# Reordering small steps of a pre-norm attention and mixture-of-experts kernel: clears on another queue, an exponential behind a copy, scatters moved and tied

## The chip, the cores and the metric

The kernel runs on one core of a Trainium2 chip. A core has a matrix engine (PE), a vector engine (DVE), a scalar engine (ACT), GpSimd (POOL) and a sync engine (SP) that only issues transfers; 16 DMA engines carry all transfers. The engines run side by side and wait for each other through semaphores. The metric is the time of one execution on the device in microseconds (us); the lower, the better. "Row" is one of the 8 sequences of the batch, numbered 0 to 7, and "tile (b, j)" is the j-th of the eight blocks of 128 tokens of row b, numbered 0 to 63 in all.

## What is computed

The input x has 8 rows of 1024 tokens with 128 features. The reference, cut to what matters:

```python
x = x + attn(layernorm(x), Wq, Wk, Wv, Wo)      # 16 heads of 8, window of 64 tokens
x = x + ffn(layernorm(x), w_router, w1, w2, bias)

# ffn: T = 8192 tokens, E = 8 experts, two experts a token, capacity 2048 an expert
scores = softmax(xf @ w_router)
expert_weights, top_experts = top_k(scores, 2)
order = argsort(flat_e, stable=True)             # a token's slot: its rank in its expert
xb = zeros((E * capacity + 1, hs)).at[slot].set(xf[src])
h = gelu(einsum('ech,ehf->ecf', xb, w1))
y = einsum('ecf,efh->ech', h, w2)
out = zeros((T, hs)).at[src].add(flat_w[order][:, None] * yv) + bias
```

So each token's normalized features are scattered to a slot of each of its two experts, in the order of the tokens, and the experts' results are added back to the tokens.

## The kernel before

The kernel has two stages. In the first, a loop over the 64 tiles does the attention and, a row later, the routing of the finished row; in the second, eight experts run over their 2048 slots each.

The attention of a tile: `scores` (L524) forms products of queries and keys on PE, and DVE takes their maxima (L565). `turn_max` turns the maxima on PE, and ACT copies them (L584). `probs` (L589) forms the products again the other way round, with the maxima subtracted (L602 to L626), and ACT takes two exponentials (L632, 1.0 us each). `attend` (L638) multiplies by the values on PE (L647), and ACT copies the result, the context and its denominators, out of PSUM (L655). In tile i the loop at L1156 issues the scores of tile i + 2, the `attend` of tile i - 1 and the `probs` of tile i. `Context` (L660) sends denominators and context by SP into another layout, where DVE inverts and scales them (L704, L705). Before a row can start, its x is normalized (`first`, L923), turned (`turn`), multiplied into queries, keys and values, and queries and keys are copied apart by SP (`spread`, L492: eight copies for each half of a row).

The order of work on PE, DVE, ACT and POOL is written out by hand: each of these engines runs its instructions in the order of the code. SP isn't in that list (L125): a planner orders its transfers by when it expects them to be ready. Three kinds of loads are held back by an explicit dependency (`after`, L92), and a tile's list `plan[i]` holds the small steps beside the attention. Of each list, what comes before the second step with a PE product runs in tile i behind `probs`; the rest, `behind`, runs in tile i + 1, after its scores and before its `attend`. The list `pairs[i]` runs in tile i + 1 between `attend` and `probs`.

The routing of a row b - 1 (class `Piece`, L750) runs in row b: `out` (the output projection), `stats`, `root` (the inverse square root by three Newton steps), `rooted`, `softmax` (whose exponential on ACT is L821), `choose` twice (the two best experts), `count` (PE counts the tokens of each expert, L857), `place` (slots, starting at L869), `slots` (indices for the scatters). In row b's tile 4, `rooted` and `softmax` are in `plan`, so they run in tile 5 ahead of the copy L655. `keep` (L804) adds the bias to the row on GpSimd and writes it to the output by SP.

GpSimd has three kinds of work. The scatters (`put`, L896, instruction L902) each write 128 tokens to `xb` in HBM; there are 128, taken in order from a queue, up to two a tile in rows 0 to 4 and three from row 5 on, each behind a named PE instruction. The second is the root of the row after next (L391 to L399), which is in `plan` of tile 2 behind the second product and so runs in tile 3, after that tile's first scatter. The third is `keep`. Ahead of all scatters `xb` must be cleared: `clears` (L310) writes zeros in 16 transfers of 528 KB, issued by ACT, one a tile in tiles 1 to 13 and then two a tile. The zeros themselves are made by GpSimd at 17 us.

At the end, row 7 is routed in two pieces of four tiles (`piece`, L1047, stepped by `go`). Behind the last `attend`, all scatters left over are issued, then the first piece's eight, then the second piece's eight; the second stage reads `xb` only when all are in.

Of the kernel before, what the change touches and what calls it, by code (L numbers as in the profile page):

```python
# [48 lines left out]
def kernel(  # L49
# [66 lines left out]
    with ExitStack() as ph:  # L116
# [193 lines left out]
        def clears():  # L310

            half = CAP // 2
            for i in range(2 * E):
                to = xb[i * half : (i + 1) * half, :].rearrange("(p n) d -> p (n d)", p=P)
                nc.scalar.dma_start(
                    out=to.rearrange("p (m k) -> p m k", m=NS // 8),
                    in_=bc_mid(zeros.rearrange("p n d -> p (n d)"), NS // 8),
                )
                yield
# [430 lines left out]
        class Piece:  # L750
# [47 lines left out]
            def rooted(self):  # L798
                self.norm.rooted()
# [4 lines left out]
            def keep(self):  # L804

                for j in range(0, self.n, 2):
                    t0, rows = self.b * L + (self.j0 + j) * P, self.rows[:, j : j + 2]
                    on = nc.vector if self.alone else nc.gpsimd
                    on.tensor_tensor(rows, rows, bc_mid(bias_sb, 2), ALU.add)  # L809
                    nc.sync.dma_start(  # L810
                        out=acc[t0 : t0 + 2 * P, :].rearrange("(j p) d -> p j d", p=P), in_=rows
                    )

            def softmax(self):
# [5 lines left out]
                nc.vector.tensor_tensor(self.pe, self.pe, bc(self.lmx, E), ALU.subtract)  # L820
                nc.scalar.activation(self.pe, self.pe, AF.Exp)  # L821

            def choose(self, k):
# [18 lines left out]
                if k == 0:  # L842
                    nc.vector.scalar_tensor_tensor(
                        pe, oh, -2.0, pe, op0=ALU.mult, op1=ALU.add
                    )
                else:
                    self.both = self.small("both", E)
                    nc.vector.tensor_tensor(
                        self.both, self.hot[:, :, 0], self.hot[:, :, 1], ALU.add
                    )  # L850
# [89 lines left out]
        def of(b, j0, what, *args):  # L940
            getattr(seconds[b, j0], what)(*args)
# [6 lines left out]
        at(0, 0, first, 1, "stats")  # L948
        at(0, 1, first, 1, "root", nc.vector)
        at(0, 1, first, 1, "rooted")  # L950
        at(0, 1, first, 1, "apply", range(NJ))
        at(0, 1, turn, 1, 0)
        at(0, 2, values, 0, 2)
        at(0, 2, queries, 1, 0)
        at(0, 3, keys, 1, 0)
        at(0, 3, spread, 1, 0)
        at(0, 3, first, 2, "stats")
        at(0, 3, turn, 1, 1)
        at(0, 4, queries, 1, 1)
        at(0, 4, first, 2, "root", nc.gpsimd)  # L960
        at(0, 5, keys, 1, 1)
        at(0, 5, values, 1, 0)
        at(0, 6, first, 2, "rooted")
# [6 lines left out]
        for b in range(1, B):  # L970
# [32 lines left out]
            for t, what, *args in (  # L1003
# [3 lines left out]
                (n + 4, "slots"), (n + 4, "keep"),  # L1007
            ):
                plan[t].append((of, (*f, what, *args)))
            for i in range(4):  # L1010
                pairs[n + i].append(partial(of, *f, "apply", range(2 * i, 2 * i + 2)))
            plan[n + 3][:0] = [(of, (*f, "count")), (of, (*f, "place"))]


        def half(b, j0, *steps):
# [8 lines left out]
                (of, *f, "softmax"),  # L1024
                (of, *f, "apply", FOUR[0]),
# [16 lines left out]

        half(6, 0, (53, 2), (54, 2), (55, 1), (56, 4), (57, 2), (58, 3))
        half(6, 4, (57, 2), (58, 2), (59, 1), (60, 4), (61, 2), (62, 3))


        def piece(j0, j1):  # L1047
# [8 lines left out]
                (of, *f, "softmax"),  # L1056
                (of, *f, "choose", 0),
# [5 lines left out]
                (put, 3 if j0 else 8),  # L1063
# [4 lines left out]
        def go(steps, n):  # L1068
            for _, (call, *args) in zip(range(n), steps):
                call(*args)  # L1070
                n -= 1
            return n == 0
# [4 lines left out]
        at(7, 7, go, ends[0], 4)  # L1077
# [78 lines left out]
        for i, (b, j) in enumerate(tiles):  # L1156
# [8 lines left out]
            def scores_ahead():  # L1165
                if i + 2 < len(tiles):
                    put(1, scores(*tiles[i + 2]))
# [42 lines left out]
        for which, n in ((0, 2), (1, 2), (0, 3), (1, 9), (0, 1), (1, 2)):  # L1210
            go(ends[which], n)

# [153 lines left out]
```

## Time and profile before

| | us |
|---|---|
| median of three runs | 763.94 (762.25 to 768.26) |
| the profiled execution | 764.12 |
| its span, first to last instruction | 762.3 |
| PE busy in the span | 637.5 |
| DVE, ACT, POOL busy | 381.9, 363.7, 375.7 |
| first attention exponential (L632) starts | 26.5 |
| last one starts (two, 1.94 together) | 444.5 |
| last scatter into `xb` starts | 493.2 |
| first expert's product on PE | 498.4 |

In the profile, an engine's busy time is the time of its own instructions; idle time is named by what ended it. A line such as "[9.14 <-DMA den<-sums]" behind an instruction says that its engine stood 9.14 us before it and that a transfer from `sums` to `den` ended the wait. PEclk is the share of its full clock that PE was granted.

### The profile page before, as it was taken

To read this page: it belongs to the slowest core of one execution; us is meant where nothing else is said; L and a number is where in the kernel's file an instruction comes from. 1 tells how busy PE (TensorE), PEld (TensorE's weight loads), DVE (VectorE), ACT (ScalarE), POOL (GpSimd) and SP (SyncE) were. 2 spreads that over 40 slices of the span, in tenths; PEclk is the share of its full clock that TensorE was granted. 3 is DMA by queue.
4 is the path that set the end of the run, shared out by engine and by line. 5 is a ranking of instruction groups with operands and counts; after the bars stand their busy time and mean duration, and the time that the engine had idled before them with its cause. 6 is when DMAs were issued, how large, how long until landed. Compare 5 with 4: busy or idle time off the path is not lost.

```text
span 762.3 us, 21779 instructions
## 1 busy us (share of the span) xinstructions
PE 637.5 (84%) x8777; PEld 470.3 (62%) x8777; DVE 381.9 (50%) x1169; ACT 363.7 (48%) x637; POOL 375.7 (49%) x431
## 2 busy tenths in 40 slices
PE   8797897989989888798887651499999999999990
PEld 7454554645545545455554430489999999898990
DVE  6754687766787778587888864221111111111010
ACT  5274556656656665475564530023444444443430
POOL 7010011342534435423424437538778787787876
PEclk9999798998999999999999975699999999999995
DMA  2444545333333434323332111146456465463433
GB/s 75 136 161 140 179 144 194 97 104 106 95 107 112 134 102 129 102 84 118 98 96 88 51 50 53 59 125 108 47 115 106 46 121 89 58 117 34 38 31 30
DMA packets 78308, 74.00 MB, mean 97 GB/s; under 512 B 13907, under 2 KB 63928, under 8 KB 77312
## 3 DMA queue, kind: packets, MB, share of 16 engines
q1 hardware_dynamic: 50944, 46.94, 20.0%
q0 software_dynamic: 22528, 16.74, 15.9%
q10 hardware_dynamic: 4736, 8.93, 3.1%
q8 instruction: 69, 1.13, 0.7%
q14 instruction: 31, 0.25, 0.1%
HBM read 19.14 MB, written 30.28 MB: 65 GB/s over the span
## 4 chain that ended last, share of the span: by engine, by line
PE 48%; DVE 12%; issue 11%; ACT 8%; POOL 6%; DMA 6%; SPq 6%; another core or an unknown queue 1%; POOLq 0%; ACTq 0%; DVEq 0%
PE hp L1274 12%; PE yp L1285 12%; PE av L647 6%; ACT pr L632 5%; PE t L619 5%; POOL out_dram L1295 4%; DVE mx L565 3%; PE s L557 2%; ACT mxt L584 2%; PE po L781 2%; DMA out_dram<-ye,dest 2%; PE t L602 2%; SPq L678 2%; PE xt L1263 2%; PE t L626 1%
## 5 line engine op out<-in xcount | busy, mean ns | idle before, releaser
L1295 POOL DMA_INDIRECT out_dram<-ye,dest x128 | 197.8, 1545 | 66.1 <-issue 27.1
L902 POOL DMA_INDIRECT xb<-xn,si x128 | 126.0, 985 | 169.9 <-PE s L557 58.3
L632 ACT ACTIVATE pr<-t 128x1024 f32<-128x1024 f32 x128 | 123.9, 1020 | 51.6 <-PE t L626 38.0
L565 DVE TENSOR_REDUCE mx<-s 128x8 f32<-128x768 f32 x128 | 116.4, 952 | 52.9 <-PE s L557 52.7
L1285 PEld LDWEIGHTS yp<-w,hT 128*128 128x128 f32 x1024 | 124.1, 192 | 9.2 <-ACT hT L1278 6.1
L1285 PE MATMUL yp<-w,hT 128*128 128x128 f32 x1024 | 125.3, 275 | 4.4 <-DVE ye L1290 3.7
L1274 PE MATMUL hp<-xts,w 128*128 128x256 f32 (+1 forms) x528 | 121.7, 373 | 0.3 <-DVE xts L1265 0.3
L1278 ACT ACTIVATE hT<-hp 128x512 f32<-128x512 f32 x128 | 76.4, 597 | 68.2 <-PE hp L1274 64.2
L1290 DVE TENSOR_TENSOR ye<-yp,gt 128x256 f32<-128x256 f32 (+1 forms) x66 | 27.1, 415 | 160.6 <-PE yp L1285 128.0
L1274 PEld LDWEIGHTS hp<-xts,w 128*128 128x128 f32 x528 | 93.3, 190 | 10.2 <-DVE xts L1265 0.6
L655 ACT COPY sums<-av 128x512 f32<-128x512 f32 x63 | 36.9, 586 | 92.6 <-PE av L647 59.6
L647 PE MATMUL av<-pr,vbd 128*32 128x128 f32 x2016 | 72.9, 287 | 3.7 <-ACT mxt L584 2.1
L619 PE MATMUL t<-qbd,kt 32*128 32x256 f32 x1024 | 73.9, 390 | 0.0
L647 PEld LDWEIGHTS av<-pr,vbd 128*32 128x32 f32 x2016 | 54.5, 114 | 24.7 <-ACT mxt L584 9.6
L557 PE MATMUL s<-kbd,qt 32*32 32x384 f32 x2048 | 62.6, 518 | 1.3 <-DMA kbd<-kt 1.3
L1265 ACT COPY xts<-xt 128x256 f32<-128x256 f32 (+1 forms) x57 | 21.0, 369 | 87.8 <-PE xt L1263 83.2
L619 PEld LDWEIGHTS t<-qbd,kt 32*128 32x128 f32 x1024 | 51.3, 193 | 3.4 <-issue 1.1
L809 POOL TENSOR_TENSOR x<-x,bias_sb 128x256 f32<-128x256 f32 x28 | 20.4, 752 | 49.8 <-ACT xn L415 48.5
L391 POOL TENSOR_SCALAR ln_h_x<-ln_v_x 128x8 f32<-128x8 f32 x6 | 1.5, 246 | 87.3 <-DVE ln_v_x L384 87.3
L541 PE MATMUL s<-ms,i 32*128 32x256 bf16 x256 | 29.8, 282 | 14.6 <-ACT pr L632 10.9
L704 DVE RECIPROCAL den<-den 128x128 f32<-128x128 f32 x39 | 36.8, 944 | 9.8 <-DMA den<-sums 8.3
L541 PEld LDWEIGHTS <-i 32*128 32x128 bf16 x256 | 10.3, 91 | 48.1 <-issue 43.5
(185 smaller groups left out, 785.0 us busy)
## 6 DMA issues: line engine op xcount, KB each, us to landing
xb<-zeros ACTq DMA_DIRECT2D x16, 528.0 KB
xe<-xb SPq DMA_DIRECT2D x7, 1056.0 KB
vbd<-vbd SPq DMA_DIRECT2D x32, 192.0 KB
kbd<-kt SPq DMA_DIRECT2D x62, 72.0 KB
qbd<-qt SPq DMA_DIRECT2D x64, 64.0 KB
out_dram<-x SPq DMA_DIRECT2D x32, 128.0 KB
w<-in_L_ffn_w_dram SPq DMA_DIRECT2D x16, 256.0 KB
x<-in_L_attn_x_dram SPq DMA_DIRECT2D x22, 128.0 KB
```

The lines of the kernel that those rows point to most:

```text
L541: nc.tensor.matmul(ends_of, lhsT=i32[quad(g), 0:4, :].rearrange("p n q -> p (n q)"), rhs=ms[quad(g)], start=True, stop=False, skip_group_c ...
L557: done = nc.tensor.matmul(place(g, slice(32 * blk, 32 * (blk + 1))), lhsT=qt[quad(g), q0 : q0 + 32], rhs=kbd[quad(g), :, c0 + 32 * blk : c ...
L565: nc.vector.tensor_reduce(out=part_of(mx, 0)[:, 2 * u : 2 * u + 2], in_=units[u][:, :, 0 : 4 * KB].rearrange("p g (r k) -> p g r k", r=4), ...
L619: nc.tensor.matmul(units[g // 2][:, g % 2, w], lhsT=kt[quad(g), q0 : q0 + P], rhs=qbd[quad(g), :, c0 : c0 + 64], start=False, stop=False, ...
L632: nc.scalar.activation(pr[:, 2 * u : 2 * u + 2], units[u], AF.Exp)
L647: last = nc.tensor.matmul(av[quad(g), k, :, w], lhsT=pair_values(vbd, 2 * j + w, g, k), rhs=pr[:, g, w, 2 * k : 2 * k + 2, :], start=True, ...
L655: nc.scalar.copy(sums[b, j // 4][:, :, j % 4], av.rearrange("p k s w q -> p (k s) (w q)"))
L902: ins = nc.gpsimd.indirect_dma_start(out=xb[:, :], out_offset=bass.IndirectOffsetOnAxis(ap=slot, axis=0), in_=row, in_offset=None, bounds_ ...
L1274: nc.tensor.matmul(hp[:, c], lhsT=ws[e][0][:, (c0 + c) * P : (c0 + c + 1) * P], rhs=xt, start=True, stop=True,)
L1278: nc.scalar.activation(hT[:, c0 : c0 + per], hp, AF.Gelu_apprx_tanh)
L1285: nc.tensor.matmul(yp[:, k, :], lhsT=hT[:, c, k * P : (k + 1) * P], rhs=ws[e][1][:, c, :], start=c == 0, stop=c == NC - 1,)
L1295: add = nc.gpsimd.indirect_dma_start(out=acc, out_offset=bass.IndirectOffsetOnAxis(ap=dests[e][:, n : n + 1], axis=0), in_=ye[:, k, :], in ...
```

## The change

- The 16 clears are issued by SP instead of ACT.
- `softmax` is cut in two: the exponential L821 becomes a step of its own, `exp`, and stands at the head of `pairs[n]`, behind the next tile's copy L655.
- `count` stays at the head of tile 7's list; `place` moves to its end, and so into the next tile.
- `keep` does two of the eight blocks in each of four tiles instead of all in one.
- In rows 1 to 5, tile 3's scatter behind the scores is left out; in row 5 also tile 3's scatter behind the context. Tile 6 gets one more behind the context in rows before 5.
- In row 0, the steps that prepare row 1 and the root of row 2 are spread over later tiles.
- At the end, `go` returns the last instruction of the steps it ran, and of the first piece's eight scatters two stand as before, two wait for the second piece's `rooted`, two for its `softmax`, two for the first `choose`.

```diff
-                nc.scalar.dma_start(
+                nc.sync.dma_start(
                     out=to.rearrange("p (m k) -> p m k", m=NS // 8),
...
-            def keep(self):
-
-                for j in range(0, self.n, 2):
+            def keep(self, tiles=None):
+
+                for j in tiles or range(0, self.n, 2):
...
-                nc.vector.tensor_tensor(self.pe, self.pe, bc(self.lmx, E), ALU.subtract)
+                return nc.vector.tensor_tensor(self.pe, self.pe, bc(self.lmx, E), ALU.subtract)
+
+            def exp(self):
                 nc.scalar.activation(self.pe, self.pe, AF.Exp)
...
-        at(0, 0, first, 1, "stats")
-        at(0, 1, first, 1, "root", nc.vector)
-        at(0, 1, first, 1, "rooted")
-        at(0, 1, first, 1, "apply", range(NJ))
-        at(0, 1, turn, 1, 0)
+        at(0, 1, first, 1, "stats")
         at(0, 2, values, 0, 2)
-        at(0, 2, queries, 1, 0)
+        at(0, 2, first, 1, "root", nc.vector)
+        at(0, 2, first, 1, "rooted")
+        at(0, 2, first, 1, "apply", FOUR[0])
+        at(0, 2, turn, 1, 0)
+        at(0, 3, queries, 1, 0)
+        at(0, 3, first, 1, "apply", FOUR[1])
         at(0, 3, keys, 1, 0)
         at(0, 3, spread, 1, 0)
-        at(0, 3, first, 2, "stats")
-        at(0, 3, turn, 1, 1)
+        at(0, 4, turn, 1, 1)
+        at(0, 4, first, 2, "stats")
         at(0, 4, queries, 1, 1)
-        at(0, 4, first, 2, "root", nc.gpsimd)
         at(0, 5, keys, 1, 1)
+        at(0, 5, first, 2, "root", nc.gpsimd)
         at(0, 5, values, 1, 0)
-        at(0, 6, first, 2, "rooted")
+        at(0, 7, first, 2, "rooted")
...
-                (n + 4, "slots"), (n + 4, "keep"),
+                (n + 4, "slots"),
+                (n + 4, "keep", (0,)), (n + 5, "keep", (2,)),
+                (n + 6, "keep", (4,)), (n + 7, "keep", (6,)),
             ):
                 plan[t].append((of, (*f, what, *args)))
+            pairs[n].append(partial(of, *f, "exp"))
...
-            plan[n + 3][:0] = [(of, (*f, "count")), (of, (*f, "place"))]
+            plan[n + 3].insert(0, (of, (*f, "count")))
+            plan[n + 3].append((of, (*f, "place")))
...
-                    put(1, scores(*tiles[i + 2]))
+                    put(0 if 1 <= b < 6 and j == 3 else 1, scores(*tiles[i + 2]))
...
-                put(1 if b >= 5 else 0, begun)
+                put(1 if b >= 5 and (b > 5 or j != 3) or j == 6 else 0, begun)
...
-        for which, n in ((0, 2), (1, 2), (0, 3), (1, 9), (0, 1), (1, 2)):
+        for which, n in ((0, 2), (1, 2), (0, 2)):
             go(ends[which], n)
+        put(2)
+        for n in (2, 1, 2):
+            put(2, go(ends[1], n))
+        put(len(puts), go(ends[1], 2))
+        go(ends[1], 3)
+        put(3)
+        go(ends[0], 1)
+        go(ends[1], 1)
```

More of the change, by code (lines that the diff above doesn't have):

```diff
@@ L798, in rooted @@
             def rooted(self):
-                self.norm.rooted()
+                return self.norm.rooted()
             def apply(self, tiles):
                 self.norm.apply(self.rows, self.xe2[:, :, 0:D], tiles)
-            def keep(self):
-                for j in range(0, self.n, 2):
+            def keep(self, tiles=None):
+                for j in tiles or range(0, self.n, 2):
                     t0, rows = self.b * L + (self.j0 + j) * P, self.rows[:, j : j + 2]
@@ L842, in choose @@
                 if k == 0:
-                    nc.vector.scalar_tensor_tensor(
+                    return nc.vector.scalar_tensor_tensor(
                         pe, oh, -2.0, pe, op0=ALU.mult, op1=ALU.add
                     )
[L846 to L850, printed above, removed]
+                self.both = self.small("both", E)
+                return nc.vector.tensor_tensor(
+                    self.both, self.hot[:, :, 0], self.hot[:, :, 1], ALU.add
+                )
             def count(self):
@@ L940, in of @@
         def of(b, j0, what, *args):
-            getattr(seconds[b, j0], what)(*args)
+            return getattr(seconds[b, j0], what)(*args)
         at(0, 0, queries, 0, 1)
@@ L1024, in half @@
                 (of, *f, "softmax"),
+                (of, *f, "exp"),
                 (of, *f, "apply", FOUR[0]),
@@ L1041, in half @@
             assert not calls
-        half(6, 0, (53, 2), (54, 2), (55, 1), (56, 4), (57, 2), (58, 3))
-        half(6, 4, (57, 2), (58, 2), (59, 1), (60, 4), (61, 2), (62, 3))
+        half(6, 0, (53, 2), (54, 2), (55, 1), (56, 5), (57, 2), (58, 3))
+        half(6, 4, (57, 2), (58, 2), (59, 1), (60, 5), (61, 2), (62, 3))
         def piece(j0, j1):
@@ L1056, in piece @@
                 (of, *f, "softmax"),
+                (of, *f, "exp"),
                 (of, *f, "choose", 0),
@@ L1062, in piece @@
                 (of, *f, "slots"),
-                (put, 3 if j0 else 8),
                 (of, *f, "keep"),
@@ L1069, in go @@
             for _, (call, *args) in zip(range(n), steps):
-                call(*args)
-                n -= 1
-            return n == 0
+                done = call(*args)
+            return done
         ends = [piece(0, 4), piece(4, 8)]
@@ L1076 @@
         at(7, 6, go, ends[0], 3)
-        at(7, 7, go, ends[0], 4)
+        at(7, 7, go, ends[0], 5)
         at(7, 7, go, ends[1], 2)
```

## The prediction

> **What bounds the kernel now.** I read the page first (busy rows, chain, groups), then the waits, then the timeline by tile, taking the start of each tile's probability exponential (ACT L632) as its beat.
>
> Page, kernel before:
>
> ```profile
> span 762.3 us, 21779 instructions
> PE 637.5 (84%) x8777; PEld 470.3 (62%) x8777; DVE 381.9 (50%) x1169; ACT 363.7 (48%) x637; POOL 375.7 (49%) x431
> q10 hardware_dynamic: 4736, 8.93, 3.1%
> ```
>
> PE carries the span, but not evenly. From 498 us the expert stage runs (264 us, and the diff doesn't touch it). Calm attention tiles beat at 5.64 to 5.72 us; the 64 tiles from 26.5 to 450 us take about 6.6 each. The excess is waiting, and the waits name it (engine and line, waited for; us in total, times, longest):
>
> ```profile
> ACT sums L655 <- DMA den<-sums: 12.3, 2, 9.1
> ACT lg L821 <- DVE lg L820: 33.9, 8, 13.9
> DVE upto L869 <- PE pc L857: 11.4, 8, 2.8
> ACT pr L632 <- remote: 5.9, 1, 5.9
> ```
>
> Each is a place the change touches. The first, in order of time (start, length, engine, line; idle before and releaser in brackets):
>
> ```profile
> 68.28 0.59 ACT L584 COPY mxt<-pm 128x512 bf16<-128x512 bf16 x1
> ...
> 74.83 2.47 SPq L676 DMA_DIRECT2D den<-sums  x4
> 77.45 0.52 ACTq L315 DMA_DIRECT2D xb<-zeros  x1
> 78.02 0.59 ACT L655 COPY sums<-av 128x512 f32<-128x512 f32 x1 [9.14 <-DMA den<-sums]
> ```
>
> ACT stands 9.14 us in front of one clear, which waits for a completion counter that an SP transfer (74.83) still holds; the context's copy L655 queues behind it. The second, in row 3's tile 5:
>
> ```profile
> 217.10 1.08 PE L647 MATMUL av<-pr,vbd 128*32 128x128 f32 x32
> 220.42 0.23 DVE L820 TENSOR_TENSOR lg<-lg,lmx 128x64 f32<-128x64 f32 x1
> 220.68 0.26 ACT L821 ACTIVATE lg<-lg 128x64 f32<-128x64 f32 x1 [2.88 <-DVE lg L820]
> 220.99 0.59 ACT L655 COPY sums<-av 128x512 f32<-128x512 f32 x1
> ```
>
> The copy could start at 218.2, when PE is done; it stands behind the logits' exponential until 220.99.
>
> **The change, part by part.** Sums are made against the profiled execution: 764.12 us, its span of 762.3 and 1.8 around it; the median of the runs shown is 763.94, so both read alike.
>
> *Clears on SP.* ACT loses 16 issues of 0.52 us and, above all, the waits in front of them. By the beats: tile 6 to 7 takes 12.04 against 5.7 (6.3), 7 to 8 takes 7.50 against 6.6 in the same place of rows 3 and 4 (0.9), 14 to 15 takes 7.38 against 5.6 (1.8), 15 to 16 takes 8.37 against 6.6 (1.8): together 10.8 us. What they cost on SP has no row. SP isn't ordered by hand: the copies of kt for row 2 go out at 129.50, before the values' transfer at 135.67 that stands earlier in the code; and the loads of x and w are held back by an explicit dependency. The clears have none but `zeros` (17.5 us), so I expect them in SP's first gaps (19.4 to 22.3, 23.7 to 28.5, 33.4 to 40.7) instead of one per tile. q10 carried 8.93 MB in 3.1% of 762.3 us, 23.6 us; a clear of 528 KB is 1.43 us of all engines, 16 are 23. Behind some 12 of them (17 us from 19.4; SP's transfers use eight completion counters in turn, so only eight are open at once) the eight copies of `spread(0, 1)`, issued at 28.5 to 33.4, would land near 44 rather than 35; scores of tile 4 read them at 39.0: 5 us. Bounds: 0 (the planner spaces them, or they fit the gaps), and 16 (all 16 ahead of the values' pair of 22.27, which the context at 33.6 reads: 11, and the copies behind it, 5). I take 5.5, by the gaps above. Net -5.3; bounds -10.8 and +5.2.
>
> Here the Trainium skill speaks against the edit. *DMA: Bandwidth & Descriptors* ("Issuing engines are not separate DMA queues") says that another issuing engine saves only the issue time: by it the gain is 16 x 0.52 = 8 us of an engine that is 48% busy, next to nothing. Its section "Queues, rings and completion order" says that engines take turns between queue rows, but keep order within one: by it a copy behind a clear now waits for all of it, where before both advanced. The row says that the saving is not issue time: 9.14 us at one clear. On the second rule the trace has no row for a clear ahead of a copy; my 5.5 is that rule's price.
>
> *The exponential behind the copy.* In each of rows 0 to 5 (their logits come a row later) the copy (0.59, next start 0.48 later) moves out from behind the exponential, but the exponential still stands ahead of the two `apply` and of the next L632: ACT's order becomes copy, wait to 220.68, exponential (0.31 to the next start), applies (0.78), L632 at 221.77 instead of 222.25. So not the 2.3 us of the copy's lateness, but 0.5, six times: -3.0. PE's queries, which wait 1.68 for the copy's buffer, come earlier at no cost. Bounds 0 (PE is late elsewhere) and -5 (row 2's slower beat after it, 7.7 against 5.7, goes too).
>
> *Scatters and GpSimd's root.* In rows 2 to 5 the scatter taken away in tile 3 is issued before the root (203.93; root from 206.48, waiting for DVE), so those behind the root stay two in rows 2 to 4:
>
> ```profile
> 210.89 1.06 POOL L902 DMA_INDIRECT xb<-xn,si  x1 [0.57 <-issue]
> 212.26 0.97 POOL L902 DMA_INDIRECT xb<-xn,si  x1 [0.30 <-issue]
> 213.03 0.59 ACT L655 COPY sums<-av 128x512 f32<-128x512 f32 x1 [3.16 <-PE t L626]
> ```
>
> PE had ended av at 211.18; ACT saw it 1.85 us late. Back-to-back scatters go with late releases, here and in row 5, where four of them (313.2 to 318.1) go with 5.9 us at L632. There the change takes one of the four: I take 1.5, a quarter. Bounds 0 and -6. The scatter given back in tile 6 stands between others 0.7 us apart: 0 taken, +2 at most. In row 5 the counts still end at 16 in tile 6, so 13 scatters are left at the end as before.
>
> *`place` behind the values, `keep` in four.* DVE waits 1.57 us for the counts in tile 7 and then needs 1.4 for `place`, so the maxima (L565, 237.21) come 1.8 after their scores and PE loses 0.66. That goes; but `place`'s 1.4 us then lies ahead of `slots` and the maxima in the next tile, where DVE has no gap. GpSimd's four additions in a row (241.03, 2.88 us) go with a DVE product of 0.91 us that elsewhere takes 0.29; one per tile spares 0.6. I take -1; bounds -5 and +3. Rows are kept up to three tiles later, so loads of x into the same buffers start later; they have a row's time: 0 (or +2 if SP stands before one).
>
> *Row 0's start.* The statistics of row 1 (DVE, 1.41 us at 30.23) leave the tile where PE waits 1.68 for maxima; root and half the normalizing move a tile on; row 1's queries and keys half a tile to a tile, their copies to SP with them, still ahead of tile 6. I take -1; bounds -3 and +2.
>
> *The end.* Thirteen scatters hold GpSimd from 452.2, then eight of the first piece to 478.8, then it idles until the second piece's slots (483.35). DVE's chain steps there at 0.70 or 1.40 us instead of 0.23:
>
> ```profile
> 475.63 0.19 DVE L834 TENSOR_REDUCE xn<-lg 128x4 f32<-128x32 f32 x1 [0.51 <-DVE lg L843]
> 476.34 0.19 DVE L836 TENSOR_TENSOR rk<-lg,xn 128x32 f32<-128x32 f32 x1 [0.52 <-DVE xn L834]
> ...
> 484.10 1.09 POOL L902 DMA_INDIRECT xb<-xn,si  x1 [5.31 <-issue]
> ```
>
> The new ties hold two scatters each for the root's end (466.7), the softmax (467.4) and the first choice (475.1); in the old run those scatters start at 471.4, 473.96 and 476.52. All three are then met, so nothing moves, unless fewer scatters at once let DVE step faster: then GpSimd, back to back, is the bound, 484.1 minus 479.1 = 5 us. Queued behind a tied scatter stand only later scatters. I take -0.8; bounds -5 and +2.
>
> Sum: -5.3 - 3.0 - 1.5 - 1 - 1 - 0.8 = -12.6, 764.1 to 751.5.
>
> **The rivals.** *Nothing gained in sum:* SP gives back what ACT gains (11 us), and only the exponential and half the rest stays: 759. For it: half-clock time follows every early wait (granted clock 0.90 from 34 to 137 us). Against: the wait at 78 us is single and large, and early tiles have idle PE.
>
> *Better:* SP's gaps hold the clears at 2 us, row 5's wait goes by 4, the end by 4: 764.1 - 8.8 - 3 - 4 - 2 - 4 = 742; with row 2 and the start as well, 738.
>
> *Slower:* SP becomes the bound in rows 0 and 1. It issues about 56 transfers a row at 0.6 us, 34 of some 50 us; the clears add 8 us of issue, and each can hold the queue until the transfer eight before it has landed, up to 16 x 1.43 = 23 in all. Copies, values and denominators then come late to PE by up to 31, of which early slack takes 10. That is +21 against -10.8 and -3: 771. It decides once SP costs more than some 18 us.
>
> **How the numbers follow.** Forecast (742 to 757) 0.50; better (738 and below to 742) 0.16; nothing in sum (757 to 765) 0.18; slower 0.16. About 1% (7.6 us) is what a measurement of this kernel can tell from no change. Faster by over 1%: 0.66; within: 0.18; slower: 0.16. The range leaves out the lower half of "better" and most of "slower": 738 to 767.
>
> **What would show it.** No ACT wait on a transfer before L655 in rows 0 and 1; clears on SP before 60 us; the kt copies of row 0 landing near 44; L632 of tile 5 half a microsecond sooner after L820 in each row; row 5's tile 4 still late, by about 4; last slots within 2 us of L632's last beat as before. Wrong if SP spaces the clears, if back-to-back scatters aren't what delays releases, or if DVE's slow steps at the end go.

## The result, and the profile after

The kernel after takes 766.57 us (median of 19 runs, 763.21 to 770.88), the kernel before, beside it, 762.25 (19 runs, 759.01 to 768.26): a ratio of 1.005, 95% interval 1.0031 to 1.0069. It is 3.8 us slower (2.4 to 5.3), where 12.6 us of gain were forecast. The profiled execution took 767.43 us.

The page of after, the lines that answer to those of before:

```profile
span 765.6 us, 21779 instructions
PE 638.2 (83%) x8777; PEld 471.0 (62%) x8777; DVE 382.6 (50%) x1169; ACT 363.6 (47%) x637; POOL 375.8 (49%) x431
q10 hardware_dynamic: 384, 0.28, 0.1%
```

Busy times are the same; the clears have left ACT's queue. The expert stage takes 263.4 us (263.2 before), so the difference lies in the attention. By rows, from the first L632 of a row to the next row's, before and after (one profile each): 59.5 to 62.4, 51.2 to 49.7, 52.5 to 51.2, 50.1 to 50.9, 50.1 to 54.8, 56.2 to 53.0, 51.5 to 51.2, 46.9 to 49.1; then from the last tile to the first expert 54.6 to 53.3.

The waits of after (engine and line, waited for; us in total, times, longest):

```profile
ACT pr L632 <- PE t L626: 49.1, 34, 9.6
ACT sums L655 <- remote: 23.9, 8, 3.8
DVE ctx L705 <- DMA ctx<-sums: 17.4, 13, 2.9
DVE den L704 <- DMA den<-sums: 15.2, 9, 5.0
DVE one L688 <- DMA one<-total: 10.0, 5, 4.7
```

ACT's 12.3 us for "den<-sums" are gone from this list. In their place VectorE waits longer for the same kind of transfer: 15.2 for den (8.3 before), 17.4 for ctx (9.6), 10.0 for one (2.9), and the copies L655 wait 23.9 us for a release that the profile can't name (5.1). (A release is the moment at which an engine learns through a semaphore that the product or transfer it waits for is done; one that comes later than the end of that product is called late here.) In the profile of before, VectorE's wait for den lies under ACT's:

```profile
78.61 0.95 DVE L704 RECIPROCAL den<-den 128x128 f32<-128x128 f32 x1 [4.90 <-DMA den<-sums]
```

The timeline of tiles (0,6) and (0,7) after shows the first exchange:

```profile
78.44 2.47 SPq L676 DMA_DIRECT2D den<-sums  x4
78.70 0.58 ACT L655 COPY sums<-av 128x512 f32<-128x512 f32 x1 [0.69 <-PE av L647]
...
82.22 0.95 DVE L704 RECIPROCAL den<-den 128x128 f32<-128x128 f32 x1 [4.96 <-DMA den<-sums]
84.83 0.29 DVE L705 TENSOR_TENSOR ctx<-ctx,den 128x128 f32<-128x128 f32 x1 [1.66 <-DMA ctx<-sums]
85.04 1.82 DVE L565 TENSOR_REDUCE mx<-s 128x8 f32<-128x768 f32 x2
86.05 0.58 PE L610 MATMUL t<-i,mt 32*128 32x128 bf16 x11 [7.20 <-DVE mx L565]
...
88.92 1.94 ACT L632 ACTIVATE pr<-t 128x1024 f32<-128x1024 f32 x2 [9.64 <-PE t L626]
```

ACT no longer stands in front of a clear; its copy runs at 78.70 after 0.69 us. But SP sends den only at 78.44, VectorE's scaling waits 4.96 us for it, the maxima stand behind the scaling, PE waits 7.20 for the maxima, and ACT waits 9.64 for PE. Tile (0,6) falls from 12.04 to 4.86 us, tile (0,7) rises from 7.50 to 13.84.

And in SP's list of after, with PE's wait behind it (of the 16 clears eight stand ahead of the copies of queries and keys, six behind them):

```profile
24.46 7.55 SPq L315 DMA_DIRECT2D xb<-zeros  x6
...
38.63 0.59 SPq L499 DMA_DIRECT2D kbd<-kt  x1
...
40.68 1.40 PE L557 MATMUL s<-kbd,qt 32*32 32x384 f32 x32 [3.59 <-DMA kbd<-kt]
```

This is the price that the prediction had put on the clears. Tile (0,1) takes 9.98 us instead of 5.64; as row 0's new order shortens tile (0,0) from 11.26 to 9.17, the two together take 2.3 us more (19.15 against 16.90).

Row 3 of after, tiles 3 to 6 (start, length, engine, line), and under it the two lines of before for the maxima of tile 5:

```profile
206.51 1.76 SPq L496 DMA_DIRECT2D qbd<-qt  x3
211.01 1.09 POOL L903 DMA_INDIRECT xb<-xn,si  x1 [0.58 <-PE av L647]
212.11 0.75 POOL L809 TENSOR_TENSOR x<-x,bias_sb 128x256 f32<-128x256 f32 x1
212.51 1.94 ACT L632 ACTIVATE pr<-t 128x1024 f32<-128x1024 f32 x2 [0.93 <-PE t L626]
212.89 0.38 SPq L810 DMA_DIRECT2D out_dram<-x  x1
213.03 0.99 POOL L903 DMA_INDIRECT xb<-xn,si  x1 [0.17 <-issue]
213.80 0.93 PE L557 MATMUL s<-kbd,qt 32*32 32x384 f32 x32
214.32 0.97 POOL L903 DMA_INDIRECT xb<-xn,si  x1 [0.30 <-issue]
216.26 1.82 DVE L565 TENSOR_REDUCE mx<-s 128x8 f32<-128x768 f32 x2 [1.14 <-PE tp_x L436]
217.41 2.17 SPq L673 DMA_DIRECT2D total<-sums  x4
...
221.45 1.91 ACT L632 ACTIVATE pr<-t 128x1024 f32<-128x1024 f32 x2
222.41 0.46 SPq L683 DMA_DIRECT2D one<-total  x1
224.26 0.97 POOL L903 DMA_INDIRECT xb<-xn,si  x1 [4.14 <-PE s L557]
225.54 0.97 POOL L903 DMA_INDIRECT xb<-xn,si  x1 [0.30 <-issue]
227.40 0.59 ACT L655 COPY sums<-av 128x512 f32<-128x512 f32 x1 [2.98 <-remote]
```

```profile
215.34 0.93 PE L557 MATMUL s<-kbd,qt 32*32 32x384 f32 x32
216.42 1.82 DVE L565 TENSOR_REDUCE mx<-s 128x8 f32<-128x768 f32 x2 [1.14 <-PE s L557]
```

Four readings. The release behind the root that was 1.85 us late in before is gone: a bias addition (212.11) now stands between the scatters, and tile 3 takes 5.80 instead of 7.08. The pair of scatters now stands at 213.03 and 214.32, and the scores that end at 214.73 reach VectorE only at 216.26, 1.53 us late (0.15 in the same place of before). SP issued three qbd copies at 206.51 and then stands until 212.89, when GpSimd has added: the write of the row holds back the fourth qbd copy, the keys, total (217.41) and one (222.41). And tile 6's given back scatter makes another pair (224.26, 225.54), with a copy that waits 2.98. Row 3 in sum: 0.8 us longer. The largest loss of a single row is row 4's 4.7 us; no lines of it are shown, but the parts below tell where it comes from: row 4 takes 55.3 us with the additions alone (e4) and 50.5 when their last write is held back (f3), against 50.1 in before.

### The profile page after: what moved, and what is told of

It reads as the page before. It is cut to its first block, busy times and chain, and to the rows that moved or that the text cites. A ratio compares the mean times of both kernels' runs of the same rounds, so it can differ in the third digit from the quotient of the medians.

```text
span 765.6 us, 21779 instructions
## 1 busy us (share of the span) xinstructions
PE 638.2 (83%) x8777; PEld 471.0 (62%) x8777; DVE 382.6 (50%) x1169; ACT 363.6 (47%) x637; POOL 375.8 (49%) x431
## 3 DMA queue, kind: packets, MB, share of 16 engines
q8 instruction: 69, 1.13, 0.7%
## 4 chain that ended last, share of the span: by engine, by line
PE 32%; issue 15%; POOL 12%; DVE 12%; ACT 11%; DMA 9%; SPq 7%; another core or an unknown queue 1%; POOLq 0%; DVEq 0%; ACTq 0%
POOL out_dram L1310 11%; ACT pr L632 7%; PE av L647 5%; PE t L619 5%; DMA out_dram<-ye,dest 5%; PE yp L1300 5%; PE hp L1289 4%; PE awake L169 3%; DVE mx L565 3%; SPq L678 2%; ACT mxt L584 2%; SPq L676 2%; PE po L781 2%; PE t L602 2%; DMA ctx<-sums 2%
## 5 line engine op out<-in xcount | busy, mean ns | idle before, releaser
L903 POOL DMA_INDIRECT xb<-xn,si x128 | 125.9, 984 | 199.7 <-PE t L626 49.3
L632 ACT ACTIVATE pr<-t 128x1024 f32<-128x1024 f32 x128 | 123.8, 1019 | 54.1 <-PE t L626 49.1
L565 DVE TENSOR_REDUCE mx<-s 128x8 f32<-128x768 f32 x128 | 116.3, 951 | 44.4 <-PE s L557 40.4
L1305 DVE TENSOR_TENSOR ye<-yp,gt 128x256 f32<-128x256 f32 (+1 forms) x66 | 27.0, 415 | 160.7 <-PE yp L1300 128.6
L655 ACT COPY sums<-av 128x512 f32<-128x512 f32 x63 | 36.8, 585 | 99.1 <-PE av L647 68.9
L619 PE MATMUL t<-qbd,kt 32*128 32x256 f32 x1024 | 78.0, 398 | 1.1 <-issue 1.0
L619 PEld LDWEIGHTS t<-qbd,kt 32*128 32x128 f32 x1024 | 53.6, 195 | 5.4 <-issue 3.2
L704 DVE RECIPROCAL den<-den 128x128 f32<-128x128 f32 x39 | 36.8, 945 | 15.2 <-DMA den<-sums 15.2
L541 PE MATMUL s<-ms,i 32*128 32x256 bf16 x256 | 28.1, 280 | 16.3 <-ACT pr L632 12.5
L602 PE MATMUL t<-i,mt 32*128 32x256 bf16 x448 | 28.9, 281 | 14.6 <-DVE mx L565 9.3
```

The source lines that it names most:

```text
L541: nc.tensor.matmul(ends_of, lhsT=i32[quad(g), 0:4, :].rearrange("p n q -> p (n q)"), rhs=ms[quad(g)], start=True, stop=False, skip_group_c ...
L565: nc.vector.tensor_reduce(out=part_of(mx, 0)[:, 2 * u : 2 * u + 2], in_=units[u][:, :, 0 : 4 * KB].rearrange("p g (r k) -> p g r k", r=4), ...
L602: nc.tensor.matmul(to, lhsT=mt[quad(g), 0, hq, :], rhs=i32[quad(g)].rearrange("p (w r) q -> p w r q", w=2), start=hq == 0, stop=False, ski ...
L619: nc.tensor.matmul(units[g // 2][:, g % 2, w], lhsT=kt[quad(g), q0 : q0 + P], rhs=qbd[quad(g), :, c0 : c0 + 64], start=False, stop=False, ...
L632: nc.scalar.activation(pr[:, 2 * u : 2 * u + 2], units[u], AF.Exp)
L903: ins = nc.gpsimd.indirect_dma_start(out=xb[:, :], out_offset=bass.IndirectOffsetOnAxis(ap=slot, axis=0), in_=row, in_offset=None, bounds_ ...
```

## The experiments

Each set of runs ran on one chip with the kernel before beside it; all ratios are against that. Before took 763.5 to 765.2 us in four sets and 744.94 on the chip of e9 to e12, called the faster chip below. Ratios are turned to us with the set's own before. "Beat 3 to 4" is from the start of L632 in a row's tile 3 to that in tile 4; a beat comes from one profile.

### One part at a time

The first seven each do one part of the change on the kernel before, or (e7) undo one in after.

**Clears on SP** alone:

```diff
-                nc.scalar.dma_start(
+                nc.sync.dma_start(
```

> Kernel before with one edit: the 16 clears are issued by SP. Prediction's step: 5.3 us faster than before (ACT's waits of 10.8 us gone, some 5 us at the copies of kt). Theory A, after the result: the wait at ACT only lay over a backlog of SP that is there anyway, so it moves: tile (0,6) falls from 12.0 to about 5, tile (0,7) rises by as much (DVE's first scaling of the context waits for the same transfer), tile (0,1) is 4 us longer; in sum +1 to +5 us. Rival B, SP becomes the bound of row 1 too: rows 0 and 1 together longer by more than 6 us.

Measured: 763.94 against 763.47, ratio 1.0008 (0.9976 to 1.0040). Tile (0,6) takes 4.86 us, (0,7) 12.70, (0,1) 9.62: theory A's mechanism. By the profiles, tiles (0,0) and (0,1) are 2.5 us longer together, (0,6) and (0,7) 2.0 shorter. In row 1 tiles 6 and 7, which took 7.38 and 8.37, take 5.06 and 6.64: there the 3.6 us of the prediction come. The row is 1.6 us shorter, as tiles 0 and 5 of it got longer.

**The exponential behind the copy** alone:

```diff
-                nc.vector.tensor_tensor(self.pe, self.pe, bc(self.lmx, E), ALU.subtract)
+                return nc.vector.tensor_tensor(self.pe, self.pe, bc(self.lmx, E), ALU.subtract)
+
+            def exp(self):
                 nc.scalar.activation(self.pe, self.pe, AF.Exp)
...
+            pairs[n].append(partial(of, *f, "exp"))
```

> Kernel before with one edit: the logits' exponential stands behind the context's copy. Prediction's step: 3.0 us faster (0.5 in each of rows 0 to 5). Rival: the copy's earlier end lets PE and GpSimd's scatter go earlier, and what follows waits anyway; no difference (within 1.5 us), with tile 4 of each row 0.5 us shorter and a later one as much longer.

Measured: 760.55 against 763.47, ratio 0.9961 (0.9939 to 0.9984): 3.0 us faster, as the prediction's step has it. From the start of the maxima L565 to that of tile 5's L632, row 3 takes 5.83 us in before (216.42 to 222.25) and 5.19 here (212.35 to 217.54): 0.64 a row, where 0.5 was taken.

**The scatters' counts** alone:

```diff
-                    put(1, scores(*tiles[i + 2]))
+                    put(0 if 1 <= b < 6 and j == 3 else 1, scores(*tiles[i + 2]))
...
-                put(1 if b >= 5 else 0, begun)
+                put(1 if b >= 5 and (b > 5 or j != 3) or j == 6 else 0, begun)
```

> Kernel before with one edit: the scatters' counts of the change (tile 3's left out in rows 1 to 5, tile 6's given back), bias additions still in one. Prediction's step: 1.5 us faster, beat from tile 3 to 4 still 7.1 us in rows 2 to 4, and tile 6 as before. Theory A, the scatter left out removes the stall of tile 3 and the one given back makes another: beat 3 to 4 about 5.8 in rows 2 to 5 (8 us gained), beat 5 to 6 up from 5.5 to 7 or more in rows 2 to 4 (2 us each): in sum 2 us faster to 2 slower. Rival B, it is the bias addition between the scatters that removed the stall: beat 3 to 4 stays at 7.1 here.

Measured: 766.40, ratio 1.0025 (0.9999 to 1.0051), 1.9 us slower. Beat 3 to 4 stays at 7.43, 7.16 and 7.00 in rows 2 to 4 and falls from 10.81 to 9.55 in row 5: as the prediction said, the pair behind the root stays, and row 5 loses a quarter. Theory A falls. Beat 5 to 6 is 1.1 longer in row 3, 0.4 in row 4 and 1.1 shorter in row 2, where before had 7.70. So the price of tile 6's given back scatter isn't shown by this run: in the five kernels with scatters, additions and exponential as in before, this beat lies anywhere from 5.5 to 7.7 in these rows. In row 5, where none is given back, it is 1.6 longer: the scatters left out in tile 3 come there, three instead of one, and what tile 3 gained is lost.

**The bias additions in four tiles** alone:

```diff
-                (n + 4, "slots"), (n + 4, "keep"),
+                (n + 4, "slots"),
+                (n + 4, "keep", (0,)), (n + 5, "keep", (2,)),
+                (n + 6, "keep", (4,)), (n + 7, "keep", (6,)),
```

> Kernel before with one edit: the bias additions (and the writes of the rows) in four tiles instead of one. Prediction's step (part of 1 us): 0.5 us faster. Theory A, the scatter left out did it: beat 3 to 4 of rows 2 to 4 stays at 7 or gets longer, since one more instruction of 0.75 us stands between GpSimd's root and the last scatter of the burst: 0 to 4 us slower. Rival B, the addition spaces the scatters: beat 3 to 4 about 5.8, 4 us faster.

Measured: 765.44, ratio 1.0029 (1.0002 to 1.0057), 2.2 us slower. Beat 3 to 4 is 5.86, 5.90 and 5.89, and 6.92 in row 5: it is the addition between the scatters that removes tile 3's stall (rival B's mechanism), but not its 4 us: beat 4 to 5 rises from 8.50, 8.21 and 8.20 to 9.25, 9.58 and 9.29, and row 4's beat 5 to 6 from 5.56 to 8.95. From the maxima to tile 5's exponential it takes the same 5.83 us as in before (212.33 to 218.16), and the maxima start 1.53 us behind their scores: the pair of scatters that had delayed ACT's copy now delays VectorE.

**`place` at the end of the list** (e5), and **row 0's new order** (e6, the lines of row 0 in the change's diff), alone:

```diff
-            plan[n + 3][:0] = [(of, (*f, "count")), (of, (*f, "place"))]
+            plan[n + 3].insert(0, (of, (*f, "count")))
+            plan[n + 3].append((of, (*f, "place")))
```

> Kernel before with one edit: the slots' positions (place) stand at the end of tile 7's list, so in the next tile. Prediction's step (the other part of 1 us): 0.5 us faster, 0.66 us of PE's wait in tile 7 gone from each row. Rival: its 1.4 us of DVE then lie ahead of the maxima of a tile in which DVE has no gap, and the rows get 0.3 to 0.7 us longer: 2 to 4 us slower.

> Kernel before with one edit: row 0's new order of the steps for row 1 and of row 2's root. Prediction's step: 1 us faster. Rival: the copies of row 1's keys and queries are later on SP, whose backlog in tiles 6 and 7 of row 0 sets the pace there; tile (0,0) about 2 us shorter, tiles 6 and 7 together 2 to 4 us longer: 0 to 2 us slower.

Measured: 1.0013 (0.9990 to 1.0037) and 0.9995 (0.9971 to 1.0018). Neither differs from before. In e6, tile (0,0) is 2.1 us shorter (9.16), tile (0,4) 1.5 longer (6.60) and tile (0,6) 1.0 longer (13.04), where ACT waits 10.14 for den instead of 9.14; row 0 takes 59.6, before 59.5.

**The old end in after**, ties taken out and the first piece's eight scatters in one (the diff is against after):

```diff
...
-        for which, n in ((0, 2), (1, 2), (0, 2)):
+        for which, n in ((0, 2), (1, 2), (0, 3), (1, 10), (0, 1), (1, 2)):
             go(ends[which], n)
-        put(2)
-        for n in (2, 1, 2):
-            put(2, go(ends[1], n))
...
```

> Kernel after with one part undone: the end as before (the first piece's eight scatters in one, the second's without ties). Prediction's step: 0.8 us slower than after, so 767.4. Rival: the new end gives the 1.3 us that one profile shows between the last tile and the first expert, 767.9; or nothing, 766.6; either way from the last exponential to the first expert's product 54.6 us as before.

Measured: 1.0065 (1.0041 to 1.0089), after 1.0050: 1.1 us for the new end, with an uncertainty of some 2.4. It agrees with the step (0.8), and with nothing gained. The profiles speak for a gain: from the last tile to the first expert the 13 with the old end on these chips take 53.7 to 57.0 us (55.5 on average; e7 56.0), the three with the new end 52.6 to 53.9 (after, f4, f6; 53.3).

### Were ACT's waits worth anything?

e1 removes them and gives SP work at the same time. Two runs keep SP out of it. First, GpSimd issues the clears (`nc.gpsimd.dma_start` in place of `nc.scalar.dma_start`):

> Kernel before with one edit: the 16 clears are issued by GpSimd, in the same tiles; neither ACT nor SP issues them. Theory A, ACT's 9 us wait only lay over SP's backlog in row 0: no gain (within 2 us), tile (0,6) about 5, tile (0,7) 12 to 13. Rival B (the prediction's ground): ACT's waits were real and SP's new work gave them back: 8 to 11 us faster.

Measured: 756.63 against 744.94, ratio 1.0141 (1.0099 to 1.0183), 10.5 us slower: neither theory. These lines of its timeline show why:

```profile
57.74 5.03 POOL L315 DMA_DIRECT2D xb<-zeros  x7
62.36 1.34 SPq L683 DMA_DIRECT2D one<-total  x1
71.27 0.55 DVE L688 RECIPROCAL one<-one 128x64 f32<-128x64 f32 x1 [11.83 <-DMA one<-total]
```

GpSimd stood in front of row 2's root until 53.98, then issued seven clears (3.8 MB) in 5 us, and a small transfer issued behind them landed almost 9 us later. The run says what clears in a burst cost, and leaves the question open. So the second leaves them on ACT, and out of the tiles in which ACT had waited:

```diff
-            for _ in range(min(i, 1) if i < 14 else 2):
+            for _ in range({1: 1, 2: 1, 3: 1, 4: 1, 8: 2, 9: 2, 10: 2, 11: 3, 12: 3}.get(i, 0)):
```

> Kernel before with the clears still issued by ACT, but none in tiles 5, 6, 7 and 13 to 15 (one each in tiles 1 to 4, two or three each in tiles 8 to 12). Theory A, ACT's waits only lay over SP's backlog: tile (0,6) falls to about 5 and tile (0,7) rises to 12 or 13, no gain (within 2 us). Rival B, the waits were worth their 10.8 us and SP's new work gave them back in e1: 7 us faster or more, tile (0,7) stays at 7.5.

Measured: 766.99 against 764.37, ratio 1.0049 (1.0026 to 1.0073). Its timeline in tiles (0,6) and (0,7):

```profile
69.56 0.58 ACT L655 COPY sums<-av 128x512 f32<-128x512 f32 x1 [0.88 <-PE av L647]
71.13 1.94 ACT L632 ACTIVATE pr<-t 128x1024 f32<-128x1024 f32 x2 [0.98 <-PE t L626]
74.22 2.48 SPq L676 DMA_DIRECT2D den<-sums  x4
78.08 0.95 DVE L704 RECIPROCAL den<-den 128x128 f32<-128x128 f32 x1 [4.20 <-DMA den<-sums]
81.98 0.29 DVE L705 TENSOR_TENSOR ctx<-ctx,den 128x128 f32<-128x128 f32 x1 [2.95 <-DMA ctx<-sums]
83.19 0.51 PE L610 MATMUL t<-i,mt 32*128 32x128 bf16 x10 [8.29 <-DVE mx L565]
```

ACT is on time, with no clear anywhere on SP, and SP sends den at the same point as before (74.22; 74.83 there). Tile (0,6) takes 4.86 and tile (0,7) 14.82, in sum 19.68; before 19.54. (Up to 1.1 us of it may be this run's own: the transfers of ctx take 5.24 us from 76.74 on, 4.14 in before, and two moved clears go out at 78.57 beside them.) So for row 0 it is shown that ACT's 9.14 us lay over a wait of VectorE for SP that ends no earlier when ACT doesn't wait. Row 1 is another case: its tiles 6 and 7 take 5.06 and 6.69, as in e1, and the row 49.2 us. The five profiles without ACT's clears there have 47.5 to 49.7 us for row 1, the eleven others on these chips 49.3 to 54.5.

### What tiles 3 to 6 wait for

**VectorE's chain in tile 5.** To e2, one more edit: in tile 5 the softmax of the last row stands ahead of the four normalizing instructions of the row after next.

```diff
-                at(b, 4, first, b + 2, "apply", FOUR[0])
...
                 plan[t].append((of, (*f, what, *args)))
+                if what == "softmax" and b + 2 < B:
+                    at(b, 4, first, b + 2, "apply", FOUR[0])
```

> Kernel before with two edits: the exponential behind the copy (as in e2_exp, 3.0 us faster), and in tile 5 of rows 1 to 5 the softmax of the last row's logits on VectorE stands ahead of the four normalizing instructions (1.1 us) of the row after next. Theory A, VectorE's chain (maxima, normalizing, softmax) sets when tile 5's exponential starts, which is why tile 3's gain was given back: 1.0 us off the beat from tile 4 to 5 in each of five rows beyond e2_exp, in sum 8 us faster than before. Rival B, the release of the context's copy or PE sets it: as e2_exp, 3 us faster.

Measured: 761.99 against 764.58, ratio 0.9974 (0.9952 to 0.9997), no better than e2. Locally theory A holds: beat 4 to 5 is 6.57 in row 2, 6.84 in row 4 and 7.47 in row 5 (7.56, 8.23 and 8.53 in e2); row 3's isn't shorter. But row 1 takes 54.5 us, 4.1 more than in e2. Whether that belongs to the edit is not settled by one profile.

**SP's stand before the write.** The additions in four tiles, with the write of tile 3's part held by a dependency on tile 4's probabilities, so that SP puts it behind one:

```diff
+                if behind:
+                    after(into.ins, done.ins)
...
+                (n + 8, "send", 6, True),
```

> Kernel before with the bias additions in four tiles as in e4_keep, but the write of the last part (tile 3's) is held back by a dependency on tile 4's probabilities, so that SP puts it behind the context's transfers. Theory A, e4_keep is slower because SP stands in front of that write until GpSimd has added, with the copies of keys, the denominators' total and one behind it: VectorE's waits for one (10.0 us in four places in e4_keep) fall to 3 us, 2 to 4 us faster than e4_keep, 762 (the tile 3 gain stays given back to VectorE's maxima, which two scatters in a row now delay). Rival B, it is the scatters and not SP: as e4_keep, 765.5, with the waits for one no shorter.

> Kernel of e4_keep once more, beside f3 on one chip. Theory A (SP stands before tile 3's write): VectorE's waits for one about 10 us, 2 us slower than before. Rival B (scatters): slower only if late releases show on this chip.

> Kernel of e9_keep_held once more, beside f2 on one chip. Theory A: no or a short wait for one, 2 to 4 us faster than f2. Rival B: the same as f2 within 1.5 us.

Measured: e9 1.0025 (1.0000 to 1.0049), on the faster chip; on one chip f2 (not held) 1.0046 (1.0023 to 1.0069) and f3 (held) 1.0048 (1.0030 to 1.0067). The hold does what it says: of VectorE's waits for one (5.3 us in f2, 3.3 in f3) only row 0's is left, which before has too (2.9), and rows 2 to 4 take 152.8 us instead of 160.7, though 5.6 of that is one tile, (4,1), with 11.25 in f2. But row 5's beat 3 to 4 is back at 10.97 (7.03 in f2), the maxima of tile 5 start 4.1 us behind tile 4's exponential in rows 2 to 4 (3.5 to 3.7 in f2), and the medians are the same. So SP's stand is a real wait, and taking it away doesn't take away the price of this part.

On the faster chip, where releases aren't late beside scatters, a part of that price can be seen. Row 3 of e9:

```profile
208.47 1.55 DVE L573 TENSOR_TENSOR mx<-mx 128x16 f32<-128x16 f32 x2
209.23 0.74 POOL L809 TENSOR_TENSOR x<-x,bias_sb 128x256 f32<-128x256 f32 x1
213.48 1.81 DVE L565 TENSOR_REDUCE mx<-s 128x8 f32<-128x768 f32 x2
```

Beside the addition VectorE's two steps L573 take 1.55 us instead of 0.41 (e10), and its chain up to the maxima has no gap to take that up: they start 3.53 us behind tile 4's exponential (209.95), 2.65 in e10, whose additions are those of before, and beat 4 to 5 is 9.44 against 8.48.

f2 and f3 have another loss in row 7. VectorE's and GpSimd's rows of f3 there:

```profile
417.20 0.74 DVE L390 TENSOR_SCALAR ln_r_f<-ln_r_f 128x4 int32<-128x4 int32 x1
417.82 0.75 POOL L809 TENSOR_TENSOR x<-x,bias_sb 128x256 f32<-128x256 f32 x1
417.85 0.76 DVE L391 TENSOR_SCALAR ln_h_f<-ln_v_f 128x4 f32<-128x4 f32 x1
```

In before the two VectorE steps take 0.17 and 0.16. Here, just ahead of the addition and beside it, they take 1.2 us more, the maxima start 1.1 us later behind their scores, and tile (7,3) takes 9.77 (7.80 before; 10.17 in f2, 9.31 in after). The Trainium skill, *SBUF — State Buffer* ("SBUF: two separate sides"), says that GpSimd and VectorE, in some of its modes, lock a shared pair of ports against each other for a whole instruction. The second step agrees: it starts with the addition and ends with it (417.85 to 418.61, the addition 417.82 to 418.57). The first is nearly over when the addition starts, so the rule read from these rows doesn't cover it.

**The pair of scatters itself.** To e8, one edit more (e11): of the two scatters behind the root the one behind the probabilities is left out, nothing is given back. And to e8 the held additions of e9 (e12).

```diff
-            put(1, done)
+            put(0 if 1 <= b < 6 and j == 3 else 1, done)
```

> Kernel of e8_exp_chain with one more edit: in tile 3 of rows 1 to 5 the scatter behind the probabilities (not the one behind the scores) is left out, nothing given back, so that no two scatters follow each other behind GpSimd's root; bias additions as before. Theory A, two scatters in a row are what delays releases: beat 3 to 4 is 5.8 in rows 2 to 4 and 6 in row 5, beat 4 to 5 6.6 to 7: some 10 to 14 us faster than before, less 2 to 4 for the scatters that are left to the end: 752 to 756. Rival B, a wait that stands behind comes up (one from SP, the maxima): as e8_exp_chain, 762.

> Kernel of e8_exp_chain with the bias additions of e9_keep_held. Theory A, the tile 3 gain is real once VectorE's chain in tile 5 is shorter and SP isn't held: beats 3 to 5 in sum 13 us instead of 15.3 in rows 2 to 4, and 4 us off row 5: 752 to 756. Rival B, the burst of scatters moves a beat on and delays the maxima: as e8_exp_chain or 2 us slower, 762 to 764.

Measured: e11 1.0019 (0.9990 to 1.0048), e12 1.0079 (1.0049 to 1.0109), on the faster chip. There the question can't be put: beat 3 to 4 is 5.72 in all of rows 1 to 5 of e10, whose scatters and additions are those of before. (What e12 loses there is in part the additions' price just shown; it isn't taken apart here.) So e11's edit again, on e2 and on another chip:

> Kernel of e2_exp (exponential behind the copy) with one more edit: in tile 3 of rows 1 to 5 the scatter behind the probabilities is left out, nothing given back, so that one scatter, not two, follows GpSimd's root. Theory A, two in a row delay releases: beat 3 to 4 is 5.8 in rows 2 to 4 instead of 7.3 and 7 or less in row 5 instead of 10.7, with the beat 4 to 5 up by about 1 (VectorE's chain): 2 to 6 us faster than e2_exp, that is 754 to 758 where before has 764. Rival B, the row's other waits take it: as e2_exp, 0.4% faster than before, or less for the scatters left to the end. On a chip without late releases: no difference from e2_exp.

Measured: 758.51 against 765.18, ratio 0.9916 (0.9882 to 0.9949): 6.4 us faster (3.9 to 9.0), so some 3.4 beyond e2's 3.0, which is theory A's size; but e2 ran on another chip, and beside f6 below (e2 with the new end, 762.17) single runs of the two overlap (755.8 to 761.6 and 757.3 to 764.1). Beat 3 to 4 is 5.79, 5.83 and 6.19 in rows 2 to 4, and 8.82 in row 5, where beat 5 to 6 takes the gain back (8.22 instead of e2's 5.68). Row 3 of f5, to be laid beside that of after:

```profile
205.41 1.06 POOL L904 DMA_INDIRECT xb<-xn,si  x1 [0.58 <-issue]
207.30 1.95 ACT L632 ACTIVATE pr<-t 128x1024 f32<-128x1024 f32 x2
207.42 0.97 POOL L904 DMA_INDIRECT xb<-xn,si  x1 [0.95 <-PE t L626]
208.74 0.93 PE L557 MATMUL s<-kbd,qt 32*32 32x384 f32 x32
209.95 1.82 DVE L565 TENSOR_REDUCE mx<-s 128x8 f32<-128x768 f32 x2 [0.31 <-PE s L557]
...
215.13 1.91 ACT L632 ACTIVATE pr<-t 128x1024 f32<-128x1024 f32 x2
```

One microsecond lies between the scatters, and the maxima start 0.28 us behind their scores. From there to the exponential it is 5.18, as in after and e2. Mean beats of rows 2 to 4, in us:

| kernel (profiles) | 3 to 4 | 4 to 5 | 5 to 6 | sum |
|---|---|---|---|---|
| additions, scatters, exponential as before (before, e1, e5, e6, f1) | 7.28 | 8.41 | 6.12 | 21.8 |
| e2, exponential | 7.49 | 8.02 | 5.82 | 21.3 |
| e3, scatters | 7.20 | 8.44 | 6.39 | 22.0 |
| e4 and f2, additions | 5.86 | 9.42 | 7.13 | 22.4 |
| f3, additions, write held | 5.90 | 9.90 | 6.28 | 22.1 |
| after, f4, e7 | 5.89 | 8.88 | 7.73 | 22.5 |
| f5, one scatter of the pair left out | 5.94 | 7.85 | 5.54 | 19.3 |

In after, tile 3's gain of 1.4 us is given back in the two tiles behind it; in f5 it stays (against e2). Single beats scatter: 5 to 6 lies between 5.5 and 7.7 in the first line.

**All releases counted.** The same can be asked of every copy L655 that waited for its product on PE, in all profiles: how long after the product's end it starts, by the number of scatters that run at that end one behind the other (less than 0.45 us apart).

| median lateness of L655, us (copies) | no scatter | one | two |
|---|---|---|---|
| 16 profiles on the other chips | 0.07 (611) | 0.74 (183) | 2.30 (68) |
| e9 to e12, the faster chip | 0.07 (127) | 0.07 (39) | 0.07 (36) |

Of the 68 beside a pair 67 come over 1.2 us late; so do all 30 exponentials L632 and all 16 maxima L565 beside one, each 1.5 in the median. VectorE's own steps are slow beside scatters too: at the end, from the second piece's softmax (L818) to its last choice (L848) 13.5 us in before, 4.1 in e9 and in e10.

**After again**, beside f2 and f3:

> Kernel after, beside f2 and f3. As it was measured: 0.5% slower than before. Theory A (SP's order costs most of it: the write of tile 3 and the clears): about 0.5% slower on a chip with and on one without late releases. Rival B (late releases beside scatters, moved on by a tile): 0.5% slower only where they show; without them as before within 0.2%.

Measured: 1.0033 (1.0011 to 1.0055). It is slower on this chip too, one with late releases; after was not run on the faster chip, so how much of its loss needs them stays open.

**The exponential with the new end:**

> Kernel of e2_exp with the end of after (the last scatters tied to the chain). By the runs so far: 0.4% for the exponential and 0.15% for the end (e7 against after): 0.5% faster than before. Rival: the end gives nothing outside after: 0.4%.

Measured: 762.17 against 765.18, ratio 0.9943 (0.9918 to 0.9969). As expected, though 0.4% lies inside as well.

## Why the prediction was wrong, by its steps

| step | taken | measured, us (95%) |
|---|---|---|
| clears on SP | -5.3 | +0.6 (-1.8 to +3.1) |
| exponential behind the copy | -3.0 | -3.0 (-4.7 to -1.2) |
| scatters | -1.5 | +1.9 (-0.1 to +3.9) |
| `place` | half of -1 | +1.0 (-0.8 to +2.8) |
| `keep` in four | half of -1 | +2.2 (+0.2 to +4.4); again +3.5 (+1.8 to +5.3) |
| row 0's start | -1 | -0.4 (-2.2 to +1.4) |
| the end | -0.8 | -1.1 (some 2.4 either way) |
| sum | -12.6 | +1.2 |
| the whole change | -12.6 | +3.8 (+2.4 to +5.3) |

The sum (with the first of `keep`'s two) and the whole agree within the parts' intervals, which together come to some 5 us either way. Three steps failed by more than their intervals: the clears (5.9 us off), the scatters (3.4) and `keep` (2.7).

- **Clears.** The step that failed is the gain of 10.8 us, and in it the 7.2 of tiles (0,6) and (0,7). "Tile 6 to 7 takes 12.04 against 5.7 (6.3)" counted the whole excess of a tile as ACT's, and did not ask what is late next when ACT's wait goes. The answer stood in the profile of before: VectorE waited 4.90 us for the same den, to 78.61, under ACT's wait. Without ACT's wait the two tiles take 17.56 (e1) to 19.68 us (f1) instead of 19.54. The other 3.6, of row 1, did come, and 1.5 to 2.0 of them stay in the row. The cost was right in kind and too large: all sixteen went out in SP's first gaps, by 50.2 us, but eight and not twelve ahead of the copies, and PE had its keys at 40.7, some 3 us sooner than named; tiles (0,0) and (0,1) take 2.5 us more in e1. So in sum nothing: it was the rival "nothing in sum" in its mechanism, and of the two rules that the prediction set against itself the first, by which only the time of issue is saved, came out right in sum.
- **Exponential.** Right in place (0.64 in row 3) and in size; that the size agrees to a tenth is luck, with an interval of 1.7 either way. (By the lines shown the copy was 2.8 us late, not 2.3; nothing hangs on it.)
- **Scatters.** Right on what the missing scatter does where it stood: nothing in rows 2 to 4, about a quarter of row 5's wait. What failed is that nothing else was counted: in row 5 the scatters left out come in tile 5, whose beat is 1.6 longer, and "0 taken, +2 at most" for the one put into a gap of 0.7 us in tile 6 overlooks that it can make a pair. In after it does (224.26 and 225.54, the copy behind it waits 2.98 us); alone, in e3, its price isn't clear of the spread.
- **`keep`.** The prediction counted what the additions cost where they were, a VectorE product of 0.91 instead of 0.29, and gave the new places no price: there they stand beside VectorE's own short steps (1.2 us more in row 7 of f3, 1.1 in row 3 of e9), send a write into SP's order ahead of the keys and the denominators, and push the pair of scatters one release further. That they also remove tile 3's stall, and row 5's (5.74 instead of 10.81 in after, where the prediction left some 4 us of it), was not foreseen; in rows 2 to 4 it gains nothing, since the maxima of tile 5 are late by what is gained.
- **`place`, row 0, the end.** All three within a measurement of nothing; `place` leans against its forecast, and the end, by the profiles, towards it.
- **The rival "slower"** (SP the bound in rows 0 and 1) isn't what happened: row 1 of after is 1.5 us shorter than before's.

Still open: why `keep` costs the same with the write held, in full, though the profile of f3 is 3.7 us shorter than that of f2 (spans 764.0 and 767.7); f1's 0.5%, more than its rows show; and what makes a release late beside scatters.

Of these kernels f5 is faster than both: 0.9916 of before, and 0.987 of after (0.9916 by 1.005, from two sets of runs).

## What to carry to other kernels

A long wait on one engine is worth what remains when it is taken away: look in the same stretch for the other engines that wait for the same late thing, and count only the difference. When small work is spread out, price it where it goes: what it sends into a queue that runs in order, and whose short steps it now runs beside. A stall made by two instructions in a row is removed by taking one of them away; moving the pair only changes who waits.

## What the runs showed of the hardware

- Two scatters 0.3 us apart go with releases that come late: of ACT's copy by 2.30 us in the median (1.85 at 213.03 in before), of VectorE's maxima by 1.5 (216.26 in after). One alone goes with 0.74 in the median (1.13 for the copy at 206.82 in f5), none with 0.07; four in a row went with 5.2 (L632 at 319.84 in before). Taking one of the two away (f5), or putting an addition between them (e4), takes the stall away.
- On the chip of e9 to e12 this doesn't appear. In before's own profile 34 of the 97 times that L655 or L632 waits for PE the release comes over 0.25 us late, nine of them over 1.5 us, all nine beside two or more scatters; in e10 none of 103 comes over 0.16 late, though a scatter lasts 984 ns in both. The largest beside scatters in e9 to e12 is 0.9 (VectorE's maxima in e11). That goes with 20 us of the whole kernel (744.94 against 763 to 765), some 6 of them between the last tile and the first expert (47.4 to 50.2 us there, 53.7 to 57.0 with the old end elsewhere); what differs in the chip, no run tells.
- Seven clears issued within 5 us by GpSimd held a small transfer of SP's queue back by almost 9 us (e10). Six of SP's own within 7.6 us, ahead of the copies, go with 3.59 us of PE's wait for keys (after).
- Beside a GpSimd addition of 0.75 us a VectorE step of 0.16 us takes 0.76 (f3, 417.85), and two that take 0.41 together take 1.55 (e9, 208.47).
